# Graph attention layer: the order of loads, the engine of the edge preparation and the buffers of q's terms in the start of the kernel

## Chip, core and metric

One core of a Trainium2 chip. The metric is the device time of one execution in microseconds. The kernel before took 2894.26 us (median of three runs, 2880.74 to 2896.91). The engines are PE (TensorE, matrix products), ACT (ScalarE), DVE (VectorE), POOL (GpSimd), and SP, which here only issues DMA transfers. Each engine executes its own instructions in their order, and waits at an instruction until what it needs is there.

## What is computed

The reference is a graph attention layer over N = 12,500 nodes with 128 features and E = 212,500 edges that are sorted by their destination, with 8 heads of 16 features:

```python
h = relu(layernorm(x))
q = h @ Wq.T + bq                     # nodes
k = edge_attr @ Wk.T + bk             # edges
v = h @ Wv.T + bv                     # nodes
qs, qd = q[src], q[dst]               # edges, by head
in_m, out_m, diag_m = sum(qs * k), sum(qd * k), sum(qs * qd)      # over the 16 features
score = (softmax_by_dst(in_m / 4) + softmax_by_dst(out_m / 4)
         + softmax_by_dst(diag_m / 4)) * edge_weight ** lam
out = x + leaky_relu(segment_sum(score * v[dst], dst) @ Wo.T + bo, 0.1)
```

## The kernel before

The work has two stages. The **start** (about 138 us) prepares tables. The **loop** then takes the edges in 420 groups of 512.

*The start over the nodes.* x is loaded into `xq` (128 partitions, 98 tiles of 128 nodes by 128 features) in nine pieces that grow from 4 to 14 tiles (L690 to L692). The nodes are worked on in 25 groups of four tiles. For a piece, `statistics` (L830) takes bn_stats of each tile and five small sums on DVE; `scale` (L848) takes the root on ACT and the reciprocal and the `shift` (L852) on DVE. For a node group, `rectify` (L863) applies normalization and relu on ACT, `turn_h` (L866) transposes on PE and copies to `hT` on ACT, and `nodes_q` (L874) multiplies by Wq on PE, adds the bias on DVE (L881) and writes the group into `q_table` in DRAM through SP (L882). A hand-written loop (L930 to L940) interleaves these: in step g it rectifies group g + 2, turns g + 1 and projects g; statistics run further ahead. When the last group is written, POOL may begin to gather rows of `q_table`.

*The start over the edges.* The numbers of the edges (`src_r`, `dst_r`, `weight`) lie as 104 rows of 2,048. `rows_in` (L605) loads one of them in three transfers, and before the change its transfers go out through POOL's queue, beside those of x, which go through SP's. The table `side` (L911) hangs the preparation into the node loop: 

- step 2, `edges_1`: DVE converts src to float (L765), PE transposes it (L749), and DVE copies it as integers to `src_i` (L750), the indices of the gathers.
- step 5 turns three weight matrices, step 6 splits the biases into three bf16 terms (L819).
- step 8, `edges_2`: POOL converts dst (L769), DVE takes the difference of neighbours, `step` (L771), and POOL makes a row of zeros and -1e30 of it (L773), which is written to `fa_d`.
- step 11, `edges_3`: the place of each edge's destination relative to its block's first (DVE, L778 and L781), reordered and cast by POOL (L784), written to `rel_d`.
- steps 14, 17, 20, `edges_4(c)`: POOL casts the weight to bf16 (L790), DVE subtracts the cast from the weight (L792), and the next step casts the rest: three terms, each written to `fa_d`.

The casts use a tile `of`, of which there are two buffers. `step` lies in the memory of `src_r` (tag "step").

*Behind the node loop* come the first nine groups' gathers on POOL (L941), the loads of edge features for six groups (`fetch_edges`, L943), and `fetch(0)` (L618), which loads what the first block needs from `rel_d` and `fa_d`. Then `terms_q` (L888) splits q into three bf16 terms for each of the 25 node groups: two casts on ACT (L898, L904), two subtractions on DVE (L899, L905), and a write of 384 KB to `q3_table` (L907). The buffer of a group's terms is one of four of its own; each third group uses one of the two buffers of `of`. Every third step carries a piece of `edges_5`.

*The loop over the edges.* A group needs 512 gathered rows of q by src, in four indirect transfers of 128 rows (L656, POOL), its edge features (turned by PE, L1107, and projected, L1117), and q of the destinations (L1126). DVE multiplies and sums by head (L1137, L1138, L1140), and scans over the sorted edges follow (L1170, L1198). Gathers run nine groups ahead of the products (LOOK = 9) into eleven buffers.

The order on each engine is the order of the program for everything that goes through `pin` (L596): it makes each instruction follow the one before it on its engine.

Of the kernel before, what the change touches and what calls it, by code (L numbers as in the profile page):

```python
# [7 lines left out]
F32 = mybir.dt.float32  # L8
BF = mybir.dt.bfloat16
I32 = mybir.dt.int32  # L10
AF = mybir.ActivationFunctionType
ALU = mybir.AluOpType
# [460 lines left out]
def ordered_path(ctx: ExitStack, tc: tile.TileContext, flag, x, src, dst, edge_attr, edge_weight,  # L473
# [122 lines left out]
    def pin(inst):  # L596

        engine = str(inst.ins.engine)
        if engine in pinned:
            tc.add_manual_dep(inst.ins, pinned[engine], mybir.DependencyInfo(  # L600
                mybir.DependencyClass.NoSync, mybir.DependencyReason.DATA), reason="in order")
        pinned[engine] = inst.ins.name
        return inst

    def rows_in(to, t, q):  # L605

        top, cut = (RW - 1) * RC, 96
        q.dma_start(to[0:cut, :], t[:cut * RC].rearrange("(r c) -> r c", c=RC))
        q.dma_start(to[cut:RW - 1, :], t[cut * RC:top].rearrange("(r c) -> r c", c=RC))
        q.dma_start(to[RW - 1:RW, :E - top], t[None, top:E])  # L610

    qqs, st, eas, behind, base_v = {}, {}, {}, {}, {}

# [66 lines left out]
    with tc.tile_pool(name="prep", bufs=1) as prep, \  # L680
# [5 lines left out]
        pin(nc.sync.dma_start(lam_sb, lam[None, :].to_broadcast([RW, 1])))  # L686
        w_in = prep.tile([P, 4, F], F32, name="w_in")
        pin(nc.sync.dma_start(w_in[:, 0, :], Wq))
        xq = prep.tile([P, NI, F], F32, name="xq")
        LOADS = [0, 2, 4] + list(range(CU, NU + 1, CU))  # L690
        for lo, hi in zip(LOADS, LOADS[1:]):
            nodes_in(xq[:, 2 * lo:2 * hi, :], lo, hi - lo, nc.sync)  # L692
            if lo == 0:
                pin(nc.sync.dma_start(bq_all, bq[None, :].to_broadcast([P, F])))
        b_row = prep.tile([1, 3, F], F32, name="b_row")
        for i, b in enumerate((bv, bk, bo)):
            pin(nc.sync.dma_start(b_row[:, i, :], b[None, :]))
# [10 lines left out]
                                  dst[None, at + BE - 1:at + (n - 1) * BE + BE:BE, None]))  # L708
        pin(nc.sync.dma_start(tops[:, T - 1:, S - 1:S], dst[None, E - 1:E, None]))

        src_r = prep.tile([RW, RC], I32, name="src_r", tag="step")
        nc.gpsimd.memset(src_r[96:, :], 0)
        rows_in(src_r, src, nc.gpsimd)

        dst_r = prep.tile([RW, RC + 2], I32, name="dst_r")
        nc.gpsimd.memset(dst_r[96:, :], N)
        nc.gpsimd.memset(dst_r[:, 0:1], -1)
        rows_in(dst_r[:, 1:RC + 1], dst, nc.gpsimd)
        pin(nc.gpsimd.dma_start(dst_r[1:, 0:1], dst[RC - 1:(RW - 1) * RC:RC, None]))
        pin(nc.gpsimd.dma_start(dst_r[:RW - 1, RC + 1:], dst[RC:(RW - 1) * RC + 1:RC, None]))  # L720
        weight = prep.tile([RW, RC], F32, name="weight")
        nc.gpsimd.memset(weight[96:, :], 1.0)
        rows_in(weight, edge_weight.rearrange("e o -> (e o)"), nc.gpsimd)
        for i, w in enumerate((Wv, Wk, Wo)):
            pin(nc.gpsimd.dma_start(w_in[:, i + 1, :], w))

# [30 lines left out]
        def fa_out(c, of):  # L757
            pin(nc.sync.dma_start(fa_d.rearrange("(r a) c e -> c r a e", a=RB)[c],
                                  of.rearrange("r (a e) -> r a e", a=RB)))

        def of_tile():
            return prep.tile([P, RC], BF, name="of", bufs=2)[:RW]

        def edges_1():
            pin(nc.vector.tensor_copy(src_f, src_r))  # L765
            turn_edges(src_f, src_i)

        def edges_2():
            pin(nc.gpsimd.tensor_copy(dst_f, dst_r))  # L769
            step = got["step"] = prep.tile([RW, RC + 1], F32, name="step", tag="step")  # L770
            pin(nc.vector.tensor_sub(step, dst_f[:, 1:], dst_f[:, :RC + 1]))  # L771
            of = of_tile()
            pin(nc.gpsimd.tensor_scalar(of, step[:, :RC], 0.0, -FAR, op0=ALU.is_gt, op1=ALU.mult))  # L773
            fa_out(0, of)

        def edges_3():
            base_c = prep.tile([RW, RB], F32, name="base_c")
            pin(nc.vector.tensor_copy(base_c, dst_f[:, 1:RC + 1:BE]))  # L778
            for a in range(RB):
                part = rel[:, a * BE:(a + 1) * BE]  # L780
                pin(nc.vector.tensor_scalar(part, part, base_c[:, a:a + 1], 1.0, op0=ALU.subtract,  # L781
                                            op1=ALU.add))
            rel_b = of_tile().rearrange("r (a e) -> r a e", a=RB)
            pin(nc.gpsimd.tensor_copy(rel_b.rearrange("r a (j p) -> r a j p", j=JN),  # L784
                                      rel.rearrange("r (a p j) -> r a j p", a=RB, j=JN)))
            pin(nc.sync.dma_start(rel_d.rearrange("(r a) e -> r a e", a=RB), rel_b))

        def edges_4(c):
            of = of_tile()
            pin(nc.gpsimd.tensor_copy(of, weight))  # L790
            if c < 2:
                pin(nc.vector.tensor_sub(weight, weight, of))  # L792
            fa_out(c + 1, of)

        def edges_5(i):
            step = got["step"]
# [91 lines left out]
        def terms_q(g):  # L888

            if g < GN:  # L890
                n = len(tiles_of(g))
                q = xq[:, g * JN:g * JN + n, :]
                if g % 3 == 2:
                    q3 = prep.tile([P, JN, 3, F], BF, name="q3", tag="of", bufs=2)
                else:
                    q3 = node.tile([P, JN, 3, F], BF, name="q3", bufs=4)
                q3 = q3s[g] = q3[:, :n]
                pin(nc.scalar.copy(q3[:, :, 0, :], q))  # L898
                pin(nc.vector.tensor_sub(q, q, q3[:, :, 0, :]))  # L899
            if g > 0:  # L900
                n = len(tiles_of(g - 1))
                q = xq[:, (g - 1) * JN:(g - 1) * JN + n, :]
                q3 = q3s.pop(g - 1)
                pin(nc.scalar.copy(q3[:, :, 1, :], q))  # L904
                pin(nc.vector.tensor_sub(q3[:, :, 2, :], q, q3[:, :, 1, :]))  # L905
                lo = (g - 1) * JN * P
                pin(nc.sync.dma_start(  # L907
                    q3_table[3 * lo:3 * (lo + n * P), :].rearrange("(u p k) f -> p u (k f)", p=P, k=6),
                    q3.rearrange("p (u k) t f -> p u (k t f)", k=2)))

        side = {2: edges_1, 5: turn_ws, 6: biases, 8: edges_2, 11: edges_3, 14: lambda: edges_4(0),  # L911
                17: lambda: edges_4(1), 20: lambda: edges_4(2)}
        turn_w(0, wq)
        parts = [(2 * lo, 2 * hi) for lo, hi in zip(LOADS, LOADS[1:])]

# [14 lines left out]
        for g in range(-2, GN):  # L930
            if g + 2 < GN:
                rectify(g + 2)
            if 0 <= g + 1 < GN:
                turn_h(g + 1)
            if g >= 0:
                nodes_q(g)
            ready(g + 4)
            measure(g + 6 + min(max(g, 0), 6))
            if g in side:
                side[g]()  # L940
        for g in range(LOOK):  # L941
            gather(g)
        for g in range(AHEAD):  # L943
            fetch_edges(g)
        fetch(0)
        for g in range(GN + 1):
            terms_q(g)
            if g % 3 == 2:
                edges_5(g // 3)
        bad = got["bad"]  # L950
# [468 lines left out]
```

## Time and profile before

| | |
|---|---|
| median of three runs | 2894.26 us |
| profiled execution | 2295.63 us |
| its span, first to last instruction | 2293.8 us |
| PE busy | 1828.4 us (80%) |
| DVE busy | 2073.1 us (90%) |
| ACT busy | 1651.9 us (72%) |
| POOL busy | 1645.2 us (72%) |
| mean granted clock of PE | 0.80 |
| first gather starts | 94.85 us |
| first matrix product of the loop (L1117) starts | 139.00 us |
| last gather starts | 2213.8 us |

The profile is of one execution. A busy share is a mean over the whole span, so it doesn't tell what bounds a stage; for that the instructions are read in order of time, with the idle time ahead of each and what ended it. POOL's busy time leaves out some 0.30 us between two gathers in which it waits for nothing that the profile shows ("issue"). The median of the runs lies 599 us above the profiled execution; both are of the same kernel.

### The profile page before, as it was taken

The page shows a single profiled execution, that of the slowest core. Times are in us where ns is not written, and L with a number is a line of the kernel's source. Part 1 is how long each engine was busy: PE and PEld are TensorE (multiplying, and loading weights), DVE is VectorE, ACT ScalarE, POOL GpSimd, SP SyncE. Part 2 cuts the span into 40 slices and gives each one's busy share as a digit, 9 for nine tenths or more (in the row PEclk, how much of TensorE's full clock was granted, in tenths as well). Part 3 has the DMA queues.
Part 4 walks back from the last instruction along what each step waited for, and adds up shares of the span by engine and source line. Part 5 has one row for each costly group of instructions (what it writes and reads, how often), then busy time and mean ns, then how long its engine had stood idle before and what let it go on. Part 6 is the DMA issues. An engine that isn't in the chain of part 4 may idle for free.

```text
span 2293.8 us, 36583 instructions
## 1 busy us (share of the span) xinstructions
PE 1828.4 (80%) x10781; PEld 1396.7 (61%) x10781; DVE 2073.1 (90%) x2180; ACT 1651.9 (72%) x3049; POOL 1645.2 (72%) x1716
## 2 busy tenths in 40 slices
PE   5437888888888887878888878888787888888876
PEld 3325666666666666666666666666666666666654
DVE  6779999999999989999988999998999899989994
ACT  5667777777767777777776777767777777777782
POOL 3577777777777777777777777777777777777740
PEclk8767878778878778887777887877888777778786
DMA  7785545545555545555545555555555545554531
GB/s 195 232 269 151 151 135 149 148 142 138 154 150 142 155 134 155 155 145 141 161 133 146 148 149 149 150 143 141 154 146 155 145 142 142 160 139 141 149 88 41
DMA packets 308901, 341.93 MB, mean 149 GB/s; under 512 B 139780, under 2 KB 227609, under 8 KB 308382
## 3 DMA queue, kind: packets, MB, share of 16 engines
q1 hardware_dynamic: 246259, 223.55, 32.5%
q0 software_dynamic: 54448, 112.96, 19.3%
q10 hardware_dynamic: 7984, 3.00, 0.5%
q8 instruction: 86, 1.41, 0.3%
q14 instruction: 124, 1.02, 0.2%
HBM read 308.22 MB, written 31.07 MB: 148 GB/s over the span
## 4 chain that ended last, share of the span: by engine, by line
PE 32%; ACT 22%; DVE 17%; issue 12%; DMA 12%; POOL 3%; SPq 0%; DVEq 0%; ACTq 0%; POOLq 0%
PE k_ps L1117 11%; DMA qq<-q_table,src_i 9%; PE eT_ps L1107 5%; DVE prod L1137 4%; ACT eT L1109 4%; PE qd_ps L1126 4%; DVE sum L1198 4%; ACT relb L1101 4%; ACT oh L1102 3%; DVE prod L1138 3%; ACT l L1160 3%; ACT qq L1128 3%; POOL qq L656 3%; PE b_ps L1226 3%; PE k_ps L1115 2%
## 5 line engine op out<-in xcount | busy, mean ns | idle before, releaser
L656 POOL DMA_INDIRECT qq<-q_table,src_i x1680 | 1608.2, 957 | 522.8 <-issue 321.5
L1140 DVE TENSOR_REDUCE lT<-prod 128x96 f32<-128x1536 f32 x420 | 736.2, 1753 | 14.4
L1117 PE MATMUL k_ps<-wk,eT 128*128 128x128 f32 x3360 | 603.9, 335 | 104.9 <-ACT eT L1109 63.7
L1117 PEld LDWEIGHTS k_ps<-wk,eT 128*128 128x128 f32 x3360 | 511.0, 233 | 252.6 <-ACT eT L1109 148.6
L1128 ACT COPY qq<-qd_ps 128x512 f32<-128x512 f32 x420 | 245.0, 583 | 443.6 <-PE qd_ps L1126 385.4
L1138 DVE TENSOR_TENSOR prod<-qq,k_ps 128x1024 f32<-128x1024 f32 x420 | 509.7, 1213 | 0.0
L1137 DVE TENSOR_TENSOR prod<-qq,qd_ps 128x512 f32<-128x512 f32 x420 | 284.2, 677 | 61.6 <-ACT qq L1128 49.2
L1126 PE MATMUL qd_ps<-win,oh 126*128 126x128 bf16 x1680 | 197.7, 251 | 167.2 <-DVE prod L1137 165.1
L1107 PE MATMUL eT_ps<-ident,ea 128*128 128x128 f32 x1680 | 325.0, 328 | 5.6 <-DVE found L955 5.6
L1101 ACT ACTIVATE relb<-relb,before 126x512 bf16<-126x512 bf16 x420 | 306.6, 730 | 0.0
L1126 PEld LDWEIGHTS <-oh 126*128 126x128 bf16 x1680 | 155.3, 114 | 202.4 <-issue 174.2
L1102 ACT ACTIVATE oh<-relb 126x512 bf16<-126x512 bf16 x420 | 264.7, 630 | 17.5 <-DMA q_table<-q 4.1
L1109 ACT COPY eT<-eT_ps 128x512 f32<-128x512 f32 x420 | 247.4, 589 | 39.5 <-PE eT_ps L1107 38.3
L1107 PEld LDWEIGHTS eT_ps<-ident,ea 128*128 128x128 f32 x1680 | 228.9, 172 | 5.9 <-DVE found L955 5.9
L1226 PE MATMUL b_ps<-ident,sum 120*128 120x120 f32 x672 | 138.7, 337 | 117.6 <-ACT l L1160 117.5
L1226 PEld LDWEIGHTS b_ps<-ident,sum 120*128 120x128 f32 x672 | 100.0, 214 | 158.2 <-ACT l L1160 135.1
L1239 PE MATMUL w_ps<-back,sel 128*126 128x144 f32 x1344 | 192.0, 297 | 0.6 <-ACT back L1227 0.6
L1115 PE MATMUL k_ps<-b,ones 3*128 3x512 bf16 x420 | 187.7, 447 | 3.9 <-DVE prod L1138 3.9
L1239 PEld LDWEIGHTS w_ps<-back,sel 128*126 128x126 f32 x1344 | 173.8, 193 | 24.8 <-issue 20.1
L1227 ACT COPY back<-b_ps 128x480 f32<-128x480 f32 x168 | 97.7, 582 | 46.1 <-PE b_ps L1226 46.1
L1170 DVE TENSOR_TENSOR_SCAN u<-l,u,far_ps 120x512 f32<-120x512 f32 x83 | 105.5, 1271 | 1.3 <-PE b_ps L1226 1.3
L1198 DVE TENSOR_TENSOR_SCAN sum<-keep,sum,up 120x512 f32<-120x512 f32 x83 | 106.0, 1277 | 0.0
(187 smaller groups left out, 1855.4 us busy)
## 6 DMA issues: line engine op xcount, KB each, us to landing
ea<-in_edge_attr_dram SPq DMA_DIRECT2D x419, 256.0 KB
relb<-rel_d SPq DMA_DIRECT2D x84, 630.0 KB
qq<-q_table,src_i POOLq DMA_INDIRECT x1680
win<-q_table SPq DMA_DIRECT2D x420, 31.5 KB
q_table<-q SPq DMA_DIRECT2D x24, 384.0 KB
fa<-fa_d SPq DMA_DIRECT2D x420, 4.0 KB
sums<-rows SPq DMA_DIRECT2D x416, 7.9 KB
q_table<-xq SPq DMA_DIRECT2D x24, 256.0 KB
```

The source lines that it names most:

```text
L656: rows = pin(nc.gpsimd.indirect_dma_start(out=qq[:, j, 0, :], out_offset=None, in_=q_table, in_offset=bass.IndirectOffsetOnAxis(ap=src_i[: ...
L1101: pin(nc.scalar.activation(d, d, AF.Abs, bias=before[:K3]))
L1102: pin(nc.scalar.activation(oh, d, AF.Relu, bias=1.0, scale=-1.0))
L1107: pin(nc.tensor.transpose(eT_ps[:, j, :], eas[g][:, j * F:(j + 1) * F], ident))
L1109: pin(nc.scalar.copy(eT, eT_ps))
L1117: pin(nc.tensor.matmul(k_ps[:, j, :], eTs[g][:, j, :], wk, start=False, stop=(j == JN - 1)))
L1126: pin(nc.tensor.matmul(qd_ps[:, j, :], ohs[g][:, j * P:(j + 1) * P], d["win"][:, s, :], start=(j == 0), stop=(j == JN - 1)))
L1128: pin(nc.scalar.copy(qqs[g][:, :, 1, :], qd_ps))
L1137: pin(nc.vector.tensor_mul(prod[:, :, 2, :], qqs[g][:, :, 0, :], qds[g]))
L1138: pin(nc.vector.tensor_mul(prod[:, :, 0:2, :], qqs[g], ks[g][:, :, None, :].to_broadcast([P, JN, 2, F])))
L1140: pin(nc.vector.tensor_reduce(lTs[t][:, :, s, :], prod.rearrange("p j i (h d) -> p j (i h) d", d=DIM), AX.X, ALU.add))
L1239: pin(nc.tensor.matmul(w_ps[:, i].rearrange("p s c -> p (s c)"), d["sel"][:, j, lo:lo + 3, :].rearrange("p s w -> p (s w)"), d["back"][:, ...
```

## The change

It concerns the start alone.

- `rows_in` pins its transfers to the order of their queue, and is called with SP's queue: the edges' numbers are now loaded behind x, in the order src, weight, dst. POOL's memsets of these tiles move ahead of the loads of x.
- A new `edges_0` at step 0: POOL converts src, makes the first two bf16 terms of the weight with the subtractions between them, and converts dst.
- `edges_1` moves from step 2 to step 9, and holds the transposes of src and the difference `step`, now on POOL.
- `edges_2` (step 15, before 8) casts the third term and writes all three; `edges_3` (step 18, before 11) makes the row of zeros and -1e30 and the relative places; their two writes move into `edges_4`, behind the gathers. The turning of the weight matrices moves from step 5 to 4.
- The edge features of six groups are loaded in steps 9 to 14 of the node loop.
- `fetch(0)` comes behind the fourth step of `terms_q`.
- The terms of q have four buffers; none is taken from `of`.

```diff
     def rows_in(to, t, q):
...
-        q.dma_start(to[0:cut, :], t[:cut * RC].rearrange("(r c) -> r c", c=RC))
+        pin(q.dma_start(to[0:cut, :], t[:cut * RC].rearrange("(r c) -> r c", c=RC)))
...
             nodes_in(xq[:, 2 * lo:2 * hi, :], lo, hi - lo, nc.sync)
             if lo == 0:
                 pin(nc.sync.dma_start(bq_all, bq[None, :].to_broadcast([P, F])))
+        rows_in(src_r, src, nc.sync)
+        rows_in(weight, edge_weight.rearrange("e o -> (e o)"), nc.sync)
+        rows_in(dst_r[:, 1:RC + 1], dst, nc.sync)
...
-        rows_in(src_r, src, nc.gpsimd)
...
+        def edges_0():
+
+            pin(nc.gpsimd.tensor_copy(src_f, src_r))
+            got["weights"] = [of_tile(), of_tile()]
+            for of in got["weights"]:
+                pin(nc.gpsimd.tensor_copy(of, weight))
+                pin(nc.gpsimd.tensor_sub(weight, weight, of))
+            pin(nc.gpsimd.tensor_copy(dst_f, dst_r))
+
         def edges_1():
-            pin(nc.vector.tensor_copy(src_f, src_r))
             turn_edges(src_f, src_i)
+            step = got["step"] = prep.tile([RW, RC + 1], F32, name="step", tag="step")
+            pin(nc.gpsimd.tensor_sub(step, dst_f[:, 1:], dst_f[:, :RC + 1]))
 
         def edges_2():
...
-            pin(nc.vector.tensor_sub(step, dst_f[:, 1:], dst_f[:, :RC + 1]))
+            for c, of in enumerate(got["weights"]):
+                fa_out(c + 1, of)
             of = of_tile()
-            pin(nc.gpsimd.tensor_scalar(of, step[:, :RC], 0.0, -FAR, op0=ALU.is_gt, op1=ALU.mult))
-            fa_out(0, of)
+            pin(nc.gpsimd.tensor_copy(of, weight))
+            fa_out(3, of)
...
-        def edges_4(c):
-            of = of_tile()
-            pin(nc.gpsimd.tensor_copy(of, weight))
-            if c < 2:
-                pin(nc.vector.tensor_sub(weight, weight, of))
-            fa_out(c + 1, of)
+
+        def edges_4():
+            fa_out(0, got["cuts"])
+            pin(nc.sync.dma_start(rel_d.rearrange("(r a) e -> r a e", a=RB), got["rel_b"]))
...
-                if g % 3 == 2:
-                    q3 = prep.tile([P, JN, 3, F], BF, name="q3", tag="of", bufs=2)
-                else:
-                    q3 = node.tile([P, JN, 3, F], BF, name="q3", bufs=4)
+                q3 = node.tile([P, JN, 3, F], BF, name="q3", bufs=4)
...
-        side = {2: edges_1, 5: turn_ws, 6: biases, 8: edges_2, 11: edges_3, 14: lambda: edges_4(0),
-                17: lambda: edges_4(1), 20: lambda: edges_4(2)}
+        side = {0: edges_0, 4: turn_ws, 6: biases, 9: edges_1, 15: edges_2, 18: edges_3}
...
+            if 9 <= g < 9 + AHEAD:
+                fetch_edges(g - 9)
         for g in range(LOOK):
             gather(g)
-        for g in range(AHEAD):
-            fetch_edges(g)
-        fetch(0)
+        edges_4()
         for g in range(GN + 1):
             terms_q(g)
+            if g == 3:
+                fetch(0)
```

More of the change, by code (lines that the diff above doesn't have):

```diff
@@ L607, in rows_in @@
         top, cut = (RW - 1) * RC, 96
-        q.dma_start(to[0:cut, :], t[:cut * RC].rearrange("(r c) -> r c", c=RC))
-        q.dma_start(to[cut:RW - 1, :], t[cut * RC:top].rearrange("(r c) -> r c", c=RC))
-        q.dma_start(to[RW - 1:RW, :E - top], t[None, top:E])
+        pin(q.dma_start(to[0:cut, :], t[:cut * RC].rearrange("(r c) -> r c", c=RC)))
+        pin(q.dma_start(to[cut:RW - 1, :], t[cut * RC:top].rearrange("(r c) -> r c", c=RC)))
+        pin(q.dma_start(to[RW - 1:RW, :E - top], t[None, top:E]))
     qqs, st, eas, behind, base_v = {}, {}, {}, {}, {}
@@ L688, in ordered_path @@
         pin(nc.sync.dma_start(w_in[:, 0, :], Wq))
+        src_r = prep.tile([RW, RC], I32, name="src_r", tag="step")
+        nc.gpsimd.memset(src_r[96:, :], 0)
+        weight = prep.tile([RW, RC], F32, name="weight")
+        nc.gpsimd.memset(weight[96:, :], 1.0)
+        dst_r = prep.tile([RW, RC + 2], I32, name="dst_r")
+        nc.gpsimd.memset(dst_r[96:, :], N)
+        nc.gpsimd.memset(dst_r[:, 0:1], -1)
         xq = prep.tile([P, NI, F], F32, name="xq")
@@ L694, in ordered_path @@
                 pin(nc.sync.dma_start(bq_all, bq[None, :].to_broadcast([P, F])))
+        rows_in(src_r, src, nc.sync)
+        rows_in(weight, edge_weight.rearrange("e o -> (e o)"), nc.sync)
+        rows_in(dst_r[:, 1:RC + 1], dst, nc.sync)
+        pin(nc.gpsimd.dma_start(dst_r[1:, 0:1], dst[RC - 1:(RW - 1) * RC:RC, None]))
+        pin(nc.gpsimd.dma_start(dst_r[:RW - 1, RC + 1:], dst[RC:(RW - 1) * RC + 1:RC, None]))
         b_row = prep.tile([1, 3, F], F32, name="b_row")
@@ L709, in ordered_path @@
         pin(nc.sync.dma_start(tops[:, T - 1:, S - 1:S], dst[None, E - 1:E, None]))
-        src_r = prep.tile([RW, RC], I32, name="src_r", tag="step")
-        nc.gpsimd.memset(src_r[96:, :], 0)
-        rows_in(src_r, src, nc.gpsimd)
[L715 to L723, printed above, removed]
         for i, w in enumerate((Wv, Wk, Wo)):
@@ L762, in of_tile @@
             return prep.tile([P, RC], BF, name="of", bufs=2)[:RW]
+        def edges_0():
[5 more added lines that the diff above has]
+            pin(nc.gpsimd.tensor_copy(dst_f, dst_r))
         def edges_1():
-            pin(nc.vector.tensor_copy(src_f, src_r))
             turn_edges(src_f, src_i)
+            step = got["step"] = prep.tile([RW, RC + 1], F32, name="step", tag="step")
+            pin(nc.gpsimd.tensor_sub(step, dst_f[:, 1:], dst_f[:, :RC + 1]))
         def edges_2():
-            pin(nc.gpsimd.tensor_copy(dst_f, dst_r))
-            step = got["step"] = prep.tile([RW, RC + 1], F32, name="step", tag="step")
-            pin(nc.vector.tensor_sub(step, dst_f[:, 1:], dst_f[:, :RC + 1]))
+            for c, of in enumerate(got["weights"]):
+                fa_out(c + 1, of)
             of = of_tile()
-            pin(nc.gpsimd.tensor_scalar(of, step[:, :RC], 0.0, -FAR, op0=ALU.is_gt, op1=ALU.mult))
-            fa_out(0, of)
+            pin(nc.gpsimd.tensor_copy(of, weight))
+            fa_out(3, of)
         def edges_3():
+            of = got["cuts"] = of_tile()
+            pin(nc.gpsimd.tensor_scalar(of, got["step"][:, :RC], 0.0, -FAR, op0=ALU.is_gt, op1=ALU.mult))
             base_c = prep.tile([RW, RB], F32, name="base_c")
@@ L782, in edges_3 @@
                                             op1=ALU.add))
[L783 removed]
+            rel_b = got["rel_b"] = of_tile().rearrange("r (a e) -> r a e", a=RB)
             pin(nc.gpsimd.tensor_copy(rel_b.rearrange("r a (j p) -> r a j p", j=JN),
                                       rel.rearrange("r (a p j) -> r a j p", a=RB, j=JN)))
[L786 to L793 removed]
+        def edges_4():
+            fa_out(0, got["cuts"])
+            pin(nc.sync.dma_start(rel_d.rearrange("(r a) e -> r a e", a=RB), got["rel_b"]))
         def edges_5(i):
```

## The prediction, made before the changed kernel had run

> **What bounds the kernel now.** I read the page's head first (span 2293.8 us; the profiled execution took 2295.63, so 1.8 lie around the span), then POOL's gather line by stage, then the start in order of time. The first view shows that the long loop runs at the pace of POOL. Columns: window, length, POOL busy (instructions), clock, DMA share, GB/s.
>
> ```profile
> 95.00:139.00 44.00, 36.08 (x27) 0.50 0.90 303
> 139.00:300.00 161.00, 121.82 (x129) 0.78 0.59 166
> ...
> 1700.00:1900.00 200.00, 151.55 (x160) 0.81 0.52 148
> ```
>
> 160 gathers in 200 us are 1.25 us each (0.94 busy, 0.30 issue), and from 139 on there is no window with fewer. Four gathers serve one group of 512 edges, so a group takes 5.0 us; VectorE, at 90%, is close behind. POOL's last gather starts at 2213.8 (its line), 80 us of tail follow. The span is therefore: start of the first gather + some 10 us lost on the first gathers + 1680 x 1.2475 + tail. The change touches none of the last three; what it can move is the first gather, at 94.85, which waits for the last write of q_table. The start in order of time shows what holds that write (start, length, engine, operation, idle time before it and its releaser):
>
> ```profile
> 25.57 2.80 DVE L835 BATCH_NORM_STATS2 stats<-xq 128x6 f32<-128x128 f32 x14 [1.84 <-DMA xq<-in_x_dram]
> ...
> 33.96 1.23 DVE L765 CAST src_r<-src_r 104x2048 f32<-104x2048 int32 x1
> ...
> 35.24 3.31 PE L749 MATMUL t_ps<-ident,src_r 104*128 104x104 f32 x16 [10.73 <-DVE src_r L765]
> ...
> 39.45 0.59 ACT L872 COPY hT<-h_ps 128x512 f32<-128x512 f32 x1 [12.97 <-PE h_ps L870]
> ...
> 65.22 1.65 ACT L863 ACTIVATE xq<-xq,shift,inv 128x128 f32<-128x128 f32 x4 [6.18 <-DVE shift L852]
> ...
> 94.85 6.81 POOL L656 DMA_INDIRECT qq<-q_table,src_i  x1 [11.10 <-DMA ea<-in_edge_attr_dram]
> ```
>
> VectorE waits for x, which shares the queues with the edges' numbers; PE waits 10.7 us for their conversion, ACT 13 us for PE; at 65.22 ACT waits for the shift of tiles 56 to 69, that is for node group 14. From there ACT sets the pace (a group each 2.03 us, 71.48 to 85.79), and 29.6 us later the first gather starts. So the question is when group 14 is rectified in the changed kernel.
>
> **Part 1, x first and less on VectorE: gain 11 us if nothing else happens.** Behind its first add (19.2) VectorE has, in the changed order up to that shift: 11 adds x 0.68 = 7.5; five chunks of statistics x 3.5 (14 bn_stats in 2.80, five small sums 0.7) = 17.5; the table shows 1.2; bias terms 1.9; four copies to src_i in 3.0; three reciprocals and shifts 1.3. Together 32.4, so 51.6; PE's transposes of src now stand behind group 9 and hold ACT's hT until about 51, so I take 54. Before: 65.2. The removed cast (1.23) and step (2.27) and the waits for x and PE are the difference. The two subtractions of weight (2.29 each) also leave VectorE, but there they lay under ACT's pace: nothing. The nine row loads move from POOL's queue to SP's, behind x. x and the weights are 6.7 MB and 7.1 MB came in the first 30 us (205, 229, 275 GB/s by tens), so x lands by 29, src by 32, weight by 35, dst by 39. On SP bases and tops (11 issues x 0.75) end near 46, when q_table's first write went before (45.88): nothing. The six loads of edge features (0.5 us of SP each, 1.5 MB) now lie between q_table writes in a stretch with DMA share 0.17 to 0.4: nothing on SP, and about 4 us of DMA leave the crowded stretch after 90.
>
> **Part 2, the work moved to POOL, and what it does to VectorE.** POOL gets the cast of src, two subtractions and the step, and its three casts of weight come forward. A cast of 104x2048 took 1.9 us (L790, mean 1901 ns). The trace has no two-input operation on POOL. Bounds: 3.8 (twice the one-input cast) and 7.1 (the slowest POOL row of this size, L773). The same subtraction took 2.27 to 2.29 on VectorE. The Trainium skill, "GPSIMD Engine Reference", section 3.1, puts a two-input elementwise operation of 2048 fp32 at 4.5 us on GpSimd against 2.29 on VectorE and advises VectorE; its VectorE figure is the trace's, so I take 4.5. So from 35 to 50 POOL reads SBUF without pause: cast 1.9, sub 4.5, cast 1.9, sub 4.5, cast of dst 1.9; the step (4.5) follows PE's transposes.
> That speaks against the change, because of these rows:
>
> ```profile
> 59.15 7.12 POOL L773 TENSOR_SCALAR of<-step 104x2048 bf16<-104x2048 f32 x1 [10.34 <-DVE step L771]
> ...
> 62.40 1.32 DVE L840 TENSOR_TENSOR sums<-stats 128x14 f32<-128x14 f32 x1
> ...
> 65.70 0.59 DVE L778 COPY base_c<-dst_r 104x4 f32<-104x4 f32 x1
> ...
> 68.15 3.93 POOL L784 CAST of<-dst_r 104x2048 bf16<-104x2048 f32 x1 [1.88 <-DVE dst_r L781]
> ...
> 70.45 1.66 DVE L852 SCALAR_TENSOR_TENSOR shift<-sums,inv 128x14 f32<-128x14 f32 x1
> ```
>
> Operations that elsewhere take 0.17 us (L841 at 63.64, L852 at 65.01) took 1.32 and 1.66; the second ended at 72.11, when POOL's cast ended (72.08), and the copy of four elements ended at 66.29 with L773 (66.27). The rule behind it: the Trainium skill, "SBUF — State Buffer", section "Who interferes with whom": a VectorE instruction with two SBUF inputs, or in a two-port mode, blocks wholly while a GpSimd instruction that reads SBUF runs. By the rows alone (1.2 to 1.5 us per meeting, two or three meetings) the loss would be 4 us; by the rule it depends on how many of VectorE's instructions slip through the gap between two POOL operations. The adds (one input in PSUM) and bn_stats (one input) go free. The five sums of a chunk and the shifts don't. At 35 VectorE comes to the sums of tiles 56 to 69, just as POOL starts.
> - Two per gap: sums pass at 36.9, 41.5 and 43.5; adds to 44.9; a shift waits until 48.1; statistics to 51; the rest as in part 1 (51.7 to 64.8, and 0.7 for the shift behind the step): group 14 at 65.5.
> - Three per gap: 64.4. One per gap: the five sums end at 50.2, group 14 at 69.5.
> I take two per gap, since each POOL operation here waits for the one before it: 65.5 against 65.2, **+0.3 us**. Both ends, 54 and 69.5, are kept.
> Behind it POOL has the third cast, the tensor_scalar of 7.1 and the reordering cast of 3.9. They wait for the writes of terms, which SP issues behind group 15's q_table write: about 73, ended by 90, and the last q_table write lands at 95. Hidden, with 5 us to spare. SP stands still about 4 us before the third term's write; q_table writes need 1.1 us and come each 2.03, so this is made good in five groups.
>
> **Part 3, four buffers of q's terms: nothing on the path, loop start -6 to +4.** Before, six served (four and two borrowed). ACT stood still for a write there:
>
> ```profile
> 103.66 0.62 ACT L898 CAST q<-xq 128x512 bf16<-128x512 f32 x1 [6.32 <-DMA q_table<-q]
> ```
>
> A buffer is held some 7.2 us (2.5 compute, 1.2 issue, 3.5 landing), so four give 1.8 us a step, against 1.56 before (18 steps from 103.66 to 131.7): +4.3. Against that, edge features and 3.5 us of waiting before L806 are gone from this stretch: up to -6. The cover: POOL may run nine groups (36 gathers) ahead, which with the slow first ones takes 10 + 36 x 1.2475 = 55 us, and the loop starts 44 us after the first gather. 11 us of delay cost nothing; beyond that each costs itself.
>
> **Sum.** +0.3 us on 2295.63, so 2295.9 profiled. The median of the runs shown (2894.26; 2880.74 to 2896.91) is 599 us above the profiled execution; no view says why, so I carry the absolute difference over: 2894.6. About 0.5% (14.5 us) can be told from no change.
>
> **Rivals.**
> - A, the forecast: the port takes back what the order gave. 2894.6, own range 2885 to 2904. Chance 0.5.
> - B, the sums slip through, or POOL's operations fall between chunks (landings earlier or later by 3 us): group 14 at 54, -11; where the loop's start counts in the timed runs, the crowded stretch gives up to 6 more: -11 to -17, 2877 to 2883. For it: three blocked rows are few, and only one cost more than 1.5 us. Against: each VectorE instruction of that kind that met a reading POOL operation was blocked. Chance 0.25.
> - C, slower: the same port, one instruction per gap (+4.3), the subtraction at 7.1 instead of 4.5 (two before the chunk is through, +5.2), and VectorE alone decides because ACT and PE stand behind it: +9.5; with four buffers binding at the loop's start +14: 2904 to 2908. It decides from the point at which POOL's block lasts beyond about 50. For it: the row of 7.1; against: that row does two operations per element. Chance 0.25.
> That x doesn't come earlier is excluded: POOL's queue carried 2.6 MB in the same 30 us.
>
> Faster by over 0.5% needs most of B's further part (0.15) and spread of the runs (0.07): 0.22. Slower: half of C and the unknown in the 599 us: 0.25. Within: 0.53. Range 2874 to 2914.
>
> **What would show it.** Right: VectorE's small sums between 35 and 50 take over 1 us each, ending with a POOL operation; POOL's subtractions take about 4.5 us; ACT's row for tile 56 starts at 64 to 66; the first gather at about 95; 160 gathers per 200 us afterwards. B: first gather near 84, sums at 0.17. C: first gather past 100, or POOL idle before its 37th gather. Wrong altogether: a gather pace other than 1.25 us, or a timed difference much larger than that of the spans.

## The result, and the profile after

The changed kernel took 2886.19 us (median of 20 runs, 2869.07 to 2908.99), the kernel before 2889.36 us in runs beside them (20 runs): ratio 0.9989, 95% interval 0.9969 to 1.0009. Timed once more on another chip, it took 2887.87 us against 2888.24 us, ratio 1.0008 (0.9987 to 1.0029; the ratios are those on record, and not always the quotient of the two medians, which would be 0.9999 here). Both intervals include 1: no difference that can be measured.

The kernel before takes about 2890 us on some chips and about 2295 us on another, and its first profile is from an execution of the second kind; so every ratio below is to the kernel before on the same chip, and starts are compared with a profile of the kernel before of the same kind (2295.63 us, or 2899.58 us from the run "before again").

The page of the changed kernel (head, busy times, and the gathers' row with mean ns, then idle time):

```profile
span 2891.8 us, 36582 instructions
...
PE 1961.0 (68%) x10781; PEld 1508.6 (52%) x10781; DVE 2093.6 (72%) x2176; ACT 1669.1 (58%) x3049; POOL 1656.2 (57%) x1711
...
L656 POOL DMA_INDIRECT qq<-q_table,src_i x1680 | 1610.1, 958 | 1079.0 <-issue 488.5
```

Busy times in us are nearly those of before; the shares are lower because the span is 598 us longer. The gathers by stage (window, length, POOL busy and count, clock, DMA share, GB/s) show where that lies:

```profile
139.00:300.00 161.00, 102.77 (x108) 0.69 0.50 143
...
1700.00:1900.00 200.00, 116.93 (x124) 0.70 0.40 113
```

124 gathers in 200 us instead of 160, that is 6.45 us a group instead of 5.0, all through the loop; one gather is still 0.94 us. It isn't the change: the kernel before, run again, showed 121 gathers in the same window, and one of the versions below ("subtractions back") showed 160 on the other kind of chip.

The start in order of time, all engines (start, length, engine, operation, idle time before it and its releaser), up to the point that the prediction watched:

```profile
38.22 4.09 POOL L770 TENSOR_TENSOR weight<-weight,of 104x2048 f32<-104x2048 f32 x1
...
40.91 1.44 DVE L847 TENSOR_TENSOR sums<-stats 128x14 f32<-128x14 f32 x1
...
42.38 1.92 POOL L769 CAST of<-weight 104x2048 bf16<-104x2048 f32 x1
42.48 1.85 DVE L850 SCALAR_TENSOR_TENSOR sums<-sums 128x14 f32<-128x14 f32 x1
...
44.38 4.07 POOL L770 TENSOR_TENSOR weight<-weight,of 104x2048 f32<-104x2048 f32 x1
44.46 4.20 DVE L829 CAST terms<-b_row 1x384 bf16<-1x384 f32 x1
48.69 2.13 DVE L830 TENSOR_TENSOR rest<-b_row,terms 1x384 f32<-1x384 f32 x1
...
57.58 1.66 PE L749 MATMUL t_ps<-ident,src_r 104*128 104x104 f32 x8 [15.76 <-DVE src_i L750]
...
60.13 0.58 ACT L879 COPY hT<-h_ps 128x512 f32<-128x512 f32 x1 [16.89 <-PE h_ps L877]
...
63.05 1.65 ACT L870 ACTIVATE xq<-xq,shift,inv 128x128 f32<-128x128 f32 x4
```

Add start and length: the small sum L847 ends at 42.35, POOL's subtraction at 42.31; L850 ends at 44.33, POOL's cast at 44.30; the cast of three bias rows (384 elements on one partition) ends at 48.66, POOL's second subtraction at 48.45; L830 ends at 50.82, POOL's next cast at 50.42. In these rows VectorE was held four times, for some 8.4 us (each length less that of its like elsewhere in this start: 0.17, 0.17, 0.35, 0.55); beside the two POOL casts before them, a sum at 34.61 and a shift at 37.37 lost another 1.3. The wait is handed on: PE stands 15.8 us until VectorE has copied the first transposes of src, and ACT 16.9 us until PE has turned the next node group. Still node group 14 is rectified at 63.05. Before again it was 67.57:

```profile
67.57 1.65 ACT L863 ACTIVATE xq<-xq,shift,inv 128x128 f32<-128x128 f32 x4 [6.63 <-DVE shift L852]
...
97.06 6.94 POOL L656 DMA_INDIRECT qq<-q_table,src_i  x1 [11.14 <-DMA ea<-in_edge_attr_dram]
```

Then the end of the node loop in the changed kernel:

```profile
71.86 7.74 SPq L758 DMA_DIRECT2D fa_d<-of  x3
...
78.85 7.12 POOL L787 TENSOR_SCALAR of<-step 104x2048 bf16<-104x2048 f32 x1
78.88 8.55 DVE L792 TENSOR_SCALAR dst_r<-dst_r,base_c 104x512 f32<-104x512 f32 x4
...
87.36 1.87 DVE L888 TENSOR_TENSOR xq<-q_ps,bq_all 128x512 f32<-128x512 f32 x3
...
90.69 0.37 ACT L879 COPY hT<-h_ps 128x256 f32<-128x256 f32 x1 [5.71 <-PE h_ps L877]
...
96.17 1.44 POOL L656 DMA_INDIRECT qq<-q_table,src_i  x1 [4.73 <-DMA rel_d<-of]
```

VectorE's four subtractions of the block bases take 8.55 us beside POOL's tensor_scalar of 7.12. Three adds of q stand behind them and run at once at 87.36; ACT waits 5.7 us for them through PE, and the first gather starts at 96.17, 33.1 us behind group 14. Before again that distance was 29.5. (The releasers that the profile names at the first gathers, writes of `rel_d` and of q's terms and loads of edge features, come behind the gathers in the program, which can't wait for them; what fits is the last q_table write, issued by 94.05 here.)

### The profile page after: what moved, and what is told of

Its sections match the earlier page's. It is cut to its first block, busy times and chain, and to the rows that moved or that the text cites. A ratio compares the mean times of both kernels' runs of the same rounds, so it can differ in the third digit from the quotient of the medians.

```text
span 2891.8 us, 36582 instructions
## 1 busy us (share of the span) xinstructions
PE 1961.0 (68%) x10781; PEld 1508.6 (52%) x10781; DVE 2093.6 (72%) x2176; ACT 1669.1 (58%) x3049; POOL 1656.2 (57%) x1711
## 4 chain that ended last, share of the span: by engine, by line
PE 38%; ACT 23%; another core or an unknown queue 15%; issue 12%; DVE 5%; DMA 5%; SPq 1%; POOL 1%; ACTq 0%; DVEq 0%; POOLq 0%
PE k_ps L1122 14%; PE eT_ps L1112 6%; ACT eT L1114 4%; ACT relb L1106 4%; ACT qq L1133 4%; PE qd_ps L1131 3%; ACT oh L1107 3%; PE b_ps L1231 3%; PE w_ps L1244 3%; PE k_ps L1120 3%; DMA qq<-q_table,src_i 2%; ACT l L1165 2%; PE d_ps L1219 1%; ACT sel L1222 1%
## 5 line engine op out<-in xcount | busy, mean ns | idle before, releaser
L1122 PE MATMUL k_ps<-wk,eT 128*128 128x128 f32 x3360 | 675.3, 363 | 610.8 <-ACT eT L1114 318.7
L1122 PEld LDWEIGHTS k_ps<-wk,eT 128*128 128x128 f32 x3360 | 574.3, 258 | 763.5 <-issue 377.3
L1145 DVE TENSOR_REDUCE lT<-prod 128x96 f32<-128x1536 f32 x420 | 736.2, 1753 | 14.4
L1112 PE MATMUL eT_ps<-ident,ea 128*128 128x128 f32 x1680 | 350.5, 347 | 3.5 <-issue 2.5
L1131 PE MATMUL qd_ps<-win,oh 126*128 126x128 bf16 x1680 | 214.1, 266 | 137.0 <-DVE prod L1142 80.7
L1131 PEld LDWEIGHTS <-oh 126*128 126x128 bf16 x1680 | 167.4, 123 | 166.7 <-DVE prod L1142 83.7
L1112 PEld LDWEIGHTS eT_ps<-ident,ea 128*128 128x128 f32 x1680 | 250.2, 185 | 2.8 <-issue 1.4
L1231 PE MATMUL b_ps<-ident,sum 120*128 120x120 f32 x672 | 154.6, 370 | 106.4 <-ACT l L1165 81.6
L1231 PEld LDWEIGHTS b_ps<-ident,sum 120*128 120x128 f32 x672 | 107.5, 215 | 160.1 <-ACT l L1165 101.0
L1075 DVE TENSOR_TENSOR h<-h,node_ps 128x512 f32<-128x512 f32 x20 | 13.7, 687 | 158.4 <-ACT h L1074 148.6
L1064 DVE TENSOR_TENSOR h<-node_ps,score 128x512 f32<-128x512 f32 x20 | 13.8, 691 | 149.5 <-remote 119.8
```

Of the source, the lines that this page charges most:

```text
L1112: pin(nc.tensor.transpose(eT_ps[:, j, :], eas[g][:, j * F:(j + 1) * F], ident))
L1122: pin(nc.tensor.matmul(k_ps[:, j, :], eTs[g][:, j, :], wk, start=False, stop=(j == JN - 1)))
L1131: pin(nc.tensor.matmul(qd_ps[:, j, :], ohs[g][:, j * P:(j + 1) * P], d["win"][:, s, :], start=(j == 0), stop=(j == JN - 1)))
L1145: pin(nc.vector.tensor_reduce(lTs[t][:, :, s, :], prod.rearrange("p j i (h d) -> p j (i h) d", d=DIM), AX.X, ALU.add))
L1231: pin(nc.tensor.transpose(b_ps[:, j, :], d["nd"][i][:, j:BE:JN], ident[:R, :R]))
```

## The experiments

All runs, with three readings of each profile. "37th" is the start of POOL's 37th gather, the first one behind the nine groups that are gathered ahead of the loop; beside it the difference to the kernel before of the same kind (151.09 or 153.23), and the timed difference, (ratio - 1) x the time before.

| kernel | before, us | group 14 | first gather | 37th | ratio (95%) | timed, us |
|---|---|---|---|---|---|---|
| before again | 2890 | 67.57 | 97.06 | 153.23 | one run | |
| changed | 2889 | 63.05 | 96.17 | 156.52, +3.3 | 0.9989 (0.9969 to 1.0009) | -3.2 |
| changed, again | 2888 | 62.57 | 95.88 | 154.73, +1.5 | 1.0008 (0.9987 to 1.0029) | +2.3 |
| no subtractions | 2890 | 55.51 | 88.62 | 145.76, -7.5 | 0.9962 (0.9944 to 0.998) | -11.0 |
| gathers later | 2890 | 62.90 | 111.83 | 165.40, +12.2 | 1.0036 (1.0019 to 1.0052) | +10.4 |
| loop later | 2890 | 63.62 | 96.90 | 156.88, +3.7 | 1.001 (0.9993 to 1.0026) | +2.9 |
| six buffers | 2295 | 62.81 | 95.94 | 156.11, +5.0 | 1.0021 (1.001 to 1.0033) | +4.8 |
| subtractions back | 2295 | 55.86 | 88.37 | 145.20, -5.9 | 0.9971 (0.9956 to 0.9986) | -6.7 |
| cuts on VectorE | 2295 | 63.18 | 90.83 | 150.70, -0.4 | 0.9989 (0.9979 to 0.9998) | -2.5 |
| x first alone | 2295 | 61.48 | 90.62 | 145.94, -5.2 | 0.9982 (0.9969 to 0.9996) | -4.1 |
| four buffers alone | 2888 | 67.15 | 96.46 | 158.39, +5.2 | 1.0016 (0.9993 to 1.0039) | +4.6 |
| biases later | 2888 | 56.70 | 93.33 | 153.50, +0.3 | 0.9992 (0.997 to 1.0015) | -2.3 |
| both | 2888 | 55.50 | 86.94 | 145.49, -7.7 | 0.9977 (0.996 to 0.9994) | -6.6 |

In most rows the timed difference is that of the 37th gather within 3 us. In "no subtractions" it differs by 3.5, inside the interval (5.2 us to each side); in the first row of the changed kernel by 6.5, a little outside it (-9.0 to +2.6). On the 2295 us chip the lead or lag of the 37th gather stays: with six buffers it is +5.0 there and +4.7 at the 301st. On the 2890 us chips POOL begins to wait for the loop at the 41st gather, and the lag can vanish in that wait: before again started it at 162.66 after a wait of 4.73 us, the changed kernel at 162.38 after one of 1.18, so that its +3.3 is -0.3 there. This fits a total that is the same.

**Before again.** The kernel before, unchanged, for a profile of the 2890 us kind.

> The kernel before, unchanged, for a second profile: the first one had a span of 2293.8 us while its timed runs took 2890. Theory 1 (POOL's gathers set the pace, 1.25 us each): the span is again near 2294. Theory 2 (that execution was unlike the timed ones): the span is near 2890, and 200 us of the loop hold some 125 gathers instead of 160, as in the changed kernel's profile; the start is the same in both: ACT rectifies tile 56 at 65, the first gather starts at 95, within 1.5 us.

Measured: 2899.58 us, 130 gathers from 400 to 600, first gather at 97.06. The second theory holds, but for the start, which is 2.2 to 2.4 us later than in the first profile. The first profile's 160 gathers in 200 us thus belong to the chip and not to the kernel: a chip on which the kernel before took 2282 to 2306 us in 66 runs shows them again below.

**Changed, again.** The changed kernel, unchanged, on another chip.

> The changed kernel as it is. Theory (the total follows the start of POOL's 37th gather): the 37th gather starts near 156.3, 5 us later than in the first profile of the kernel before (151.1), so where that kernel takes about 2295 us this one takes 2299 to 2301, ratio 1.0015 to 1.0025, about that of the run with six buffers; where it takes about 2890 us, 0.998 to 1.0005. Rival (the changed kernel gains a little at any pace): ratio 0.998 to 0.9995.

The chip was of the 2890 us kind, and 1.0008 with its interval (0.9987 to 1.0029) holds both theories. The 37th gather came 1.5 us later than before again, where the theory had counted on some 3.

**No subtractions.** POOL's subtractions of the weight are left out, so that the second and third term of the weight equal the first.

```diff
-                pin(nc.gpsimd.tensor_sub(weight, weight, of))
```

> The changed kernel without POOL's two subtractions of the weight (the second and third term then equal the first, which the output shows). If a reading POOL operation holds up VectorE: POOL's block in front ends at 42 instead of 50.4, the conversion of the biases on VectorE loses its wait (4.2 us to 0.4), ACT's wait for PE falls from 16.9 us to about 9, tile 56 is rectified at 56 to 58 instead of 63, and the first gather starts at about 90 instead of 96. If the wait came from the transfers or from PE instead: tile 56 stays at 63. Time: the gather's start passing to the end in full gives 0.998 of the kernel before less what the change itself gave, some 2881 us; not passing on, no difference.

The rows that answer (all engines in order of time, of this kernel):

```profile
55.51 1.65 ACT L869 ACTIVATE xq<-xq,shift,inv 128x128 f32<-128x128 f32 x4
...
88.62 1.44 POOL L656 DMA_INDIRECT qq<-q_table,src_i  x1 [4.74 <-DMA rel_d<-of]
```

Group 14 comes 7.5 us earlier, the first gather as much, and the time is 11.0 us under the kernel before. VectorE's lengths account for it: its sums, the shift and the bias terms from 34.6 on take 7.6 us less than in the changed kernel, the bias terms alone 1.8 instead of 7.2. So two subtractions of 4.1 us on POOL cost the path 7.5 us, though nothing on the path waits for their results. And the distance from group 14 to the first gather stays 33.1: the second loss has another cause.

**Gathers later.** Eleven memsets on POOL ahead of the gathers.

```diff
+        for _ in range(11):
+            pin(nc.gpsimd.memset(weight[96:, :], 1.0))
         for g in range(LOOK):
             gather(g)
```

> The changed kernel with eleven memsets of 1.8 us (20 us) on POOL just ahead of the first gather, which then starts at 116 instead of 96. Theory 1 (the gathers' start sets the end): 20 us longer, ratio 1.006. Theory 2 (in the timed runs the products set the pace, 6.4 us a group, and POOL, able to do a group in 5.0, catches up): 0 to 3 us longer, ratio 0.999 to 1.000.

**Loop later.** Ten copies on ACT ahead of the loop.

```diff
+        for _ in range(10):
+            pin(nc.scalar.copy(xq[:, 16:32, :], xq[:, 0:16, :]))
```

> The changed kernel with ten copies of 128x2048 on ACT (about 2.2 us each by the 0.59 us of 128x512, 20 to 22 in all) between the terms of q and the loop. Theory 1: nine groups of gathers lie ahead, so some 10 us are covered: 10 us longer, ratio 1.002. Theory 2 (the loop's start sets the end): 20 to 22 us longer, ratio 1.006.

In "gathers later" the first gather starts 15.7 us later than in the changed kernel (part of the memsets lay in the 4.7 us that POOL waited there anyway), and the total goes from -3.2 to +10.4 us against before: 13.6 of 15.7, give or take 7.5 by the two intervals. So the start of the gathers reaches the end nearly in full, at the slower pace too; why it does there, where POOL idles between gathers all through the loop, isn't shown.

In "loop later" the loop's first product comes 15.4 us later (163.55 against 148.12). The 37th gather moves by 0.4 us, but the 41st then waits for a product of the loop:

```profile
169.91 0.94 POOL L656 DMA_INDIRECT qq<-q_table,src_i  x1 [8.34 <-PE k_ps L1124]
```

It starts 7.5 us later than in the changed kernel. So the lead of the gathers hides about half of the delay, much as the first theory had it. The total, +2.9, is 6.1 us above the changed kernel's, again give or take 7.5: by the times alone, no cost and the 7.5 us can't be told apart.

**Six buffers.** The changed kernel with the six buffers of q's terms that the kernel before had.

```diff
-                q3 = node.tile([P, JN, 3, F], BF, name="q3", bufs=4)
+                if g % 3 == 2:
+                    q3 = prep.tile([P, JN, 3, F], BF, name="q3", tag="of", bufs=2)
+                else:
+                    q3 = node.tile([P, JN, 3, F], BF, name="q3", bufs=4)
```

> The changed kernel with six buffers for the terms of q, as before the change (each third group borrows one of the two of the edges' casts). If four buffers set the pace of the terms: the later steps go from 1.6 us to 1.25 each, ACT's waits for q_table's writes become rarer, and the loop's first product starts 4 to 7 us earlier than 148. The first gather stays at 96. Time, if the first gather's start sets the end: ratio 0.998 to 0.999, as with the change; if the loop's start does: 0.9965.

**Four buffers alone.** The kernel before with the reverse of that edit, and nothing else.

> The kernel before with four buffers of q's terms instead of six, nothing else. First theory (terms at the pace of four buffers hold POOL's gathers, one gather to each step of the terms): first gather unmoved near 95, some ten gathers of 1.3 to 1.45 us instead of 0.94, 37th gather 2 to 4 us later, loop's first product some 4 us later, ratio 1.001 to 1.002. Rival (as predicted: only the loop's start moves, and that lies under POOL's lead): 37th gather unmoved within 1 us, ratio 0.9995 to 1.0005.

With four buffers the terms of q and the gathers fall in step. The profile of "four buffers alone":

```profile
126.52 1.37 POOL L656 DMA_INDIRECT qq<-q_table,src_i  x1 [0.30 <-issue]
126.82 0.62 ACT L895 CAST q<-xq 128x512 bf16<-128x512 f32 x1 [0.55 <-DMA q_table<-q]
...
128.20 1.38 POOL L656 DMA_INDIRECT qq<-q_table,src_i  x1 [0.30 <-issue]
128.51 0.62 ACT L895 CAST q<-xq 128x512 bf16<-128x512 f32 x1 [0.55 <-DMA q_table<-q]
```

Both advance by 1.68 us: ACT waits for the write that frees a buffer (0.55), and each gather takes 1.37 instead of 0.94. Eleven gathers in a row take 1.1 to 1.4 us here, and eleven in the changed kernel. The same stretch with six buffers:

```profile
102.33 11.26 POOL L656 DMA_INDIRECT qq<-q_table,src_i  x1 [0.30 <-issue]
...
126.38 0.95 POOL L656 DMA_INDIRECT qq<-q_table,src_i  x1 [0.30 <-issue]
...
126.49 0.62 ACT L911 CAST q<-xq 128x512 bf16<-128x512 f32 x1
```

Gathers at 0.95, no wait on ACT, and the loop's first product at 144.17 instead of 148.12. But one gather took 11.26 us here, and the 37th came at 156.11, where the changed kernel had it (156.52 and 154.73). So six buffers bought 4 us of loop start, which gains nothing, and no gather. The expected ratio was 0.998 to 0.999; with 4.8 us above before (interval 2.3 to 7.6) this version is slower, clear of the noise, so on the 2295 us chip the changed order with six buffers doesn't gain but loses 0.2%. "Four buffers alone" came out as its first theory had it: the loop's first product 6.1 us later than before again, the 37th gather 5.2 us later. But its ratio includes 1, and its long gather (11.63 us) alone could be the cause. From the first to the 37th gather it is 56.8 to 61.9 us with four buffers ("gathers later" left out, 53.6) and 55.3 to 60.2 with more. Whether the buffers cost the gathers anything on balance stays open.

**Subtractions back.** x first and src converted on POOL as in the change; `step`, the cuts (L787) and the subtractions of the weight on VectorE, spread over the steps 11 to 17 of the node loop, with the writes of their results spread too and three buffers `of`.

```diff
-            pin(nc.gpsimd.tensor_sub(step, dst_f[:, 1:], dst_f[:, :RC + 1]))
+            pin(nc.vector.tensor_sub(step, dst_f[:, 1:], dst_f[:, :RC + 1]))
...
-        side = {0: edges_0, 4: turn_ws, 6: biases, 9: edges_1, 15: edges_2, 18: edges_3}
+        side = {0: edges_0, 4: turn_ws, 6: biases, 9: edges_1, 11: lambda: (cuts(), cast(1)), 12: lambda: less(1),
+                13: lambda: (fa_out(0, got["cuts"]), cast(2)), 14: lambda: (fa_out(1, got[1]), less(2)),
+                16: lambda: cast(3), 17: lambda: (fa_out(2, got[2]), places()),
+                19: lambda: fa_out(3, got[3]), 21: rel_out}
```

> A version made of both: x first and src turned at step 9 as in the change, but the subtractions, the step and the row of zeros and -1e30 on VectorE in steps 11 to 17, where ACT sets the pace; POOL only casts (1.9 us each, and 3.9), and the writes are spread over the later steps so that SP doesn't stand still. If reading POOL operations are what took the gain: tile 56 is rectified at 55 to 58, no VectorE instruction of the start waits over 2 us, the first gather starts at 85 to 88, and the time is 10 to 12 us below the kernel before, ratio 0.996. If the start of the gathers doesn't matter in the timed runs: ratio 0.999 or above.

**Both.** The same, and each third group's terms in one of the three buffers `of` again: seven in all, six in the words of what was expected.

> The version with step, cuts and subtractions of weights back on VectorE, and six buffers of q's terms instead of four. Theory (the 37 first gathers share the DMA queues with the terms' writes; six buffers bring the terms and the loop forward, not the gathers): first gather at 88.4, 37th at 144 to 146, loop's first product near 131 to 133, ratio 0.9965 to 0.9975, the same as with four within its interval. Rival (four buffers cost POOL's pace): 37th gather at 141 to 142, ratio 0.995 to 0.996.

The rows of "subtractions back" (all engines):

```profile
55.86 1.65 ACT L867 ACTIVATE xq<-xq,shift,inv 128x128 f32<-128x128 f32 x4
...
88.37 1.41 POOL L656 DMA_INDIRECT qq<-q_table,src_i  x1 [10.98 <-DMA q_table<-q]
```

Group 14 at 55.86 and 55.50, first gather at 88.37 and 86.94, and 6.7 and 6.6 us less than the kernel before, on two chips of the two kinds. Here the work is all done that the change does, and the gain of "no subtractions" is kept for the most part; the 10 to 12 us that were expected of "subtractions back" aren't reached (interval 3.2 to 10.1). With seven buffers the loop's first product came at 124.49, 10.8 us earlier than with four (135.27), but neither the 37th gather (145.49 against 145.20) nor the ratio changed: an earlier loop gains nothing. "Both" is also faster than the changed kernel on the same chip, 2881.93 against 2887.87 us; the difference of the two ratios, 0.0031, is more than their intervals put together as independent errors, 0.0027.

**Cuts on VectorE.** One instruction of the changed kernel, the tensor_scalar of 7.12 us, goes from POOL to VectorE.

```diff
-            pin(nc.gpsimd.tensor_scalar(of, got["step"][:, :RC], 0.0, -FAR, op0=ALU.is_gt, op1=ALU.mult))
+            pin(nc.vector.tensor_scalar(of, got["step"][:, :RC], 0.0, -FAR, op0=ALU.is_gt, op1=ALU.mult))
```

> The changed kernel with one operation moved: the row of zeros and -1e30 (7.12 us on POOL) on VectorE, by the rows of 104x2048 there 1.2 to 2.3 us. If POOL's long operation is what holds the relative places on VectorE: these take about 2 us instead of 8.55, ACT's wait of 5.7 us near the end of the node loop goes, the first gather starts at 90 to 92 instead of 96, ratio 0.9965 to 0.9975. If VectorE were held by something else: 8.5 us stay, and the ratio is 0.999.

```profile
63.18 1.65 ACT L870 ACTIVATE xq<-xq,shift,inv 128x128 f32<-128x128 f32 x4
...
80.18 1.68 DVE L792 TENSOR_SCALAR dst_r<-dst_r,base_c 104x512 f32<-104x512 f32 x4
...
90.83 1.06 POOL L656 DMA_INDIRECT qq<-q_table,src_i  x1 [2.38 <-DMA q_table<-xq]
```

Group 14 is where it was in the changed kernel; L792 takes 1.68 instead of 8.55, and the first gather starts 27.7 us behind group 14 instead of 33.1. This one instruction costs 5.5 us there, more than the whole second loss (3.6 against before again): the rest of the change gains some 2 us behind group 14. The ratio, 0.9989, gained less than expected (0.9965 to 0.9975); the changed kernel itself was not timed on this chip.

**x first alone.** The kernel before with only the loads of the edges' numbers moved behind x, on SP's queue.

> The kernel before with the order of loads alone: the edges' numbers on SP's queue behind x, everything else as before (src is turned at step 2). If the gain of the order comes from PE no longer standing behind the turning of src, this gives none, since src lands at 33 and step 2 waits for it as it did: the first gather at 95 to 98 (97 before), ratio 0.999 to 1.001. If x's earlier arrival by itself counts: the first gather 3 us earlier or more, ratio 0.998 or less.

Group 14 at 61.48 against 65.22, first gather at 90.62 against 94.85, timed -4.1 (interval -7.1 to -0.9). So x's earlier arrival counts by itself, without moving the turning of src, and the first theory is out. By the times the order of loads alone gives some 60% of the gain of "subtractions back" on the same chip; with such intervals that share is rough.

**Biases later.** The bias terms of the changed kernel are made in step 19 instead of 6.

```diff
-        side = {0: edges_0, 4: turn_ws, 6: biases, 9: edges_1, 15: edges_2, 18: edges_3}
+        side = {0: edges_0, 4: turn_ws, 9: edges_1, 15: edges_2, 18: edges_3, 19: biases}
```

> The changed kernel with the bias terms made behind node group 19 instead of behind group 6, so that VectorE doesn't stand at them while POOL works on the weights. Theory (VectorE's wait at the port delays node group 14): VectorE comes 4 to 6 us earlier to the next adds; group 14 is rectified at 57 to 59 instead of 63, first gather near 91 to 92, 37th gather 4 us earlier, ratio to the changed kernel 0.998 to 0.9985. Rival (the next operation of VectorE takes the wait over): group 14 within 1.5 us of 63, ratio to the changed kernel 0.9995 to 1.0005.

```profile
56.70 1.65 ACT L870 ACTIVATE xq<-xq,shift,inv 128x128 f32<-128x128 f32 x4
...
74.37 7.13 POOL L787 TENSOR_SCALAR of<-step 104x2048 bf16<-104x2048 f32 x1
74.46 0.68 DVE L888 TENSOR_TENSOR xq<-q_ps,bq_all 128x512 f32<-128x512 f32 x1
75.06 6.64 DVE L829 CAST terms<-b_row 1x384 bf16<-1x384 f32 x1
...
81.57 3.76 POOL L795 CAST of<-dst_r 104x2048 bf16<-104x2048 f32 x1
...
81.74 4.00 DVE L830 TENSOR_TENSOR rest<-b_row,terms 1x384 f32<-1x384 f32 x1
...
93.33 1.08 POOL L656 DMA_INDIRECT qq<-q_table,src_i  x1 [8.00 <-DMA q_table<-xq]
```

Half hit. Group 14 comes 6.3 us earlier, as the theory had it, so the bias terms carried most of the first loss. (They took 7.2 us in their old place, 1.8 of it their own work; a sum at 48.78, now beside POOL's subtraction, takes over 1.1 of the wait.) But in its new place the same cast meets POOL's next two long instructions and stands for 6.64 us, its subtraction for 4.00, and the first gather comes only 2.8 us earlier, at 93.33. Not every VectorE instruction is held: at 74.46 an add with one input in PSUM runs in its 0.68 us beside the same POOL instruction. The timing doesn't separate this kernel from the changed one.

## Why the prediction was right, and where it was wrong

It said 2894.6 us, 0.3 above the kernel before, and no difference that can be told. That is what was measured, and with the mechanism that it named: VectorE, held beside POOL, takes back what the order gives. But the size came out by luck, as its steps show:

- **The bound.** Right that the start of the gathers decides ("gathers later": 13.6 of 15.7 us) and that an earlier loop gains nothing. The working said that 11 us of delay of the loop cost nothing and more costs itself; of the 15.4 us in "loop later" 7.5 reached POOL, where it would have 4.4. Its sum of the span (94.85 + 10 + 1680 x 1.2475 + 80) is 2280.7, 13 us short of the 2293.8; only differences were used, so nothing hung on it.
- **The first gathers.** The prediction held that the change doesn't touch the 10 us lost on them. From the first to the 37th it took 60.4 us (58.9 in the second profile) instead of 56.2: another 2.7 to 4.2 us lost. Why is open.
- **The gather's pace, 1.25 us.** It had been named as what would show the prediction wrong altogether. It was 1.25 on one chip and 1.5 to 1.65 on two. The 599 us that no view explained, and that were carried over, are this. That the sum held all the same is luck in part: it was made for a loop at POOL's pace, and the timed loop ran at another.
- **Part 1, group 14 at 54 if nothing else happens.** Right within 2 us: 55.51 without the subtractions, 55.86 with them on VectorE, where POOL's casts still hold VectorE for 2 to 3 us.
- **Part 2, the port, +11.5 us.** Right in kind; the subtractions cost 7.5. POOL's subtraction takes 4.07 to 4.09 us, not 4.5 (the Trainium skill, "GPSIMD Engine Reference", section 3.1), and that of `step` 3.60. Three of the small sums pass together at 42.3, not two. On the other side the list of what is blocked was too short. It had the sums and shifts, and counted the bias terms at 1.9 us; they took 7.2 (44.46 to 51.71). The rule that the prediction quoted (the Trainium skill, "SBUF — State Buffer", "Who interferes with whom") names casts between SBUF tiles among what can enter the two-port modes, and the prediction's own fence had such a row, the copy of four elements that ended with POOL. It was not applied to the bias cast. That the adds and bn_stats go free is shown (0.68 at 74.46; 14 bn_stats in 2.79 at 38.09 beside POOL's subtraction). "Blocks wholly" is too strong for one case: in the prediction's fence the sum at 62.40 ended at 63.72, 4.57 us into POOL's tensor_scalar of 7.12, and the next four sums ran in 0.17 us each beside it. Before again (4.56) and "x first alone" (4.57) show the same. So it isn't so that each such instruction beside a reading POOL operation was blocked, as the prediction argued against its rival B.
- **"Hidden, with 5 us to spare".** This is the step that failed. It asked whether POOL's last three operations end before the last q_table write lands, and not which VectorE instructions run beside them. The subtraction of the block bases does, and holds the last adds of q, so these operations delay the very write that was to hide them: 5.5 us ("cuts on VectorE"). SP stood still 7.7 us and not 4, but in "cuts on VectorE" it stood 7.8, and the nine q_table writes behind it were through in 8.4 us, against 14.4 in the changed kernel: SP had made it good when nothing else held the writes.
- **Part 3.** A step of the terms takes about 1.65 us, predicted 1.8. Four buffers against more move the loop's start by 4.0, 6.1 and 10.8 us in three pairs of runs (the first and the last across the two kinds of chip), predicted 4.3; on the total no cost could be measured. Not foreseen was that gathers slow down in step with the terms; what this costs on balance is the point left open above.

So +0.3 was a sum of errors that cancel. Against before again group 14 came 4.5 us earlier (63.05 against 67.57) instead of 0.3 later; 3.6 us were lost from there to the first gather (33.1 against 29.5) and 4.2 from there to the 37th, instead of none; and what was left, +3.3, vanished where POOL waits for the loop. Rival B's mechanism, the sums slipping through, didn't occur; but had POOL not been given the subtractions, its place for group 14 and about its -11 us would have come, with the first gather at 88.6 and not near 84.

## What to carry to other kernels

When work is moved to POOL, list every VectorE instruction that runs beside it and takes two inputs from SBUF, or is a copy, cast or tensor_scalar between SBUF tiles, however small: a cast of 384 elements stood for 4.2 and 6.6 us. "Hidden" must be asked of the engine's neighbours too, not only of the engine's own results. And moving a blocked instruction helps only if its new place is free of long POOL instructions. Here giving POOL the one-input casts and VectorE the rest was worth 0.2 to 0.3% against the kernel before, where the change was worth nothing that could be measured.

## What the runs showed of the hardware that was not expected

- The same kernel takes 2890 us on two chips and 2295 us on a third. On the two a group takes 6.1 to 6.6 us instead of 5.0, with the granted clock at 0.71 to 0.72 instead of 0.80 to 0.81; one gather is still 0.94 us, and POOL's, PE's and ACT's pauses are spread over the whole loop. The cause wasn't found; in the start the two profiles of the kernel before differ by some 2 us.
- Gathers of 128 rows, 0.94 us otherwise, take 1.1 to 1.4 us while ACT and VectorE advance at about 1.65 us a step ("four buffers alone" and the changed kernel), and 0.94 while they advance at 1.25 ("six buffers"). Which holds which isn't shown.
- The longest of the first gathers takes 4.0 us (the changed kernel, again) to 12.4 us ("both"), as a rule in another place in each order.
- Two-input sums on VectorE got through 4.57 us after the start of POOL's tensor_scalar of 7.12 us, while copies, casts and tensor_scalars on VectorE stood to its end (66.29 against 66.27 in the kernel before). Beside POOL's subtractions and casts the two-input instructions stood to the end too.
